# A Mamba time-step projection widened to 128 rows, and eight SiLU gates put into later steps

## The chip, the core and the metric

The kernel runs on one core of one Trainium2 chip. A core has five engines that run side by side and meet through semaphores: TensorE (matmuls; PE in the profile, its weight loads PEld), VectorE (DVE), ScalarE (ACT), GpSimd (POOL) and SyncE (SP), which here only starts DMAs. Each engine works off its own list of instructions in order. Matmul results land in PSUM[...]; all other tiles lie in SBUF, over 128 partitions. The metric is the device time of one execution in microseconds (us).

## What is computed

A layer of three parts on 16 sequences of 128 rows and 512 features, in float32: cross-attention over 2048 context rows per sequence, a Mamba block with an MLP, and an FFN with a gate. The change touches the Mamba block alone. Cut to what matters:

```python
xz = einsum('bld,ed->ble', Z, in_proj_w)
x, z = split(xz, 2)                        # 1024 channels each
x = silu(causal_conv(x, conv_w, conv_b))
dt, Bm, Cm = split(einsum('bld,ed->ble', x, x_proj_w), [32, 48])
dt = softplus(einsum('blr,dr->bld', dt, dt_proj_w) + dt_proj_b)
h = exp(dt * A) * h + dt * Bm * x          # scanned over the 128 rows, 16 states a channel
y = (h . Cm) + x * D
y = y * silu(z)
out = einsum('bld,ed->ble', y, out_proj_w)
```

The time-step projection, `dt_proj_w`, contracts over 32 values only.

## The kernel before

**Steps.** One loop over `u` runs the whole kernel (L1151 to L1221 of the file). A step of the attention phase, `u` from 0 to 255, handles one sequence, one of four context blocks of 512 rows and one of four groups of four heads. There are 256 of them; the tail, `u` from 256 on, does the rest of the Mamba work and the FFN. The order in which a step issues its instructions is written by hand, and each engine keeps it:

1. DMA loads; the first half of the scan decays (`decays(g, r, 0)`, ScalarE).
2. `scores` (TensorE, four matmuls of 32 rows each at four places of the array, into the four banks), then `weighted` of the step before (TensorE), `maxima` (VectorE, L306), `x_products` (TensorE, L236), `exps` (ScalarE, L316).
3. Inputs of the next step's scan (GpSimd, L631) and sums of context blocks (`t1` to `t4`, GpSimd, L228); `silu_third`; first half of the scan (VectorE: L666, L669, and L645 which clears the state's first column); second half of the decays (L652), which waits for that clearing.
4. `turn`: 16 transposes of the exponentials (TensorE, L329) into the four banks, copied out as `pT` by ScalarE (banks 0, 1 and 3, L334) and VectorE (bank 2, L332); second half of the scan.
5. The lists `middle`, `late`, `after` and `inner`: work that is put at a given step. An item of `late` uses TensorE and gets a bank, the first one bank 0, the second bank 1, and so on; it must wait until `pT` has been copied out of that bank, and the next step's scores must wait until its result has been read.
6. `y_products` (TensorE, L236) and their sums; `silu_second` (VectorE).

**Mamba work.** Sequences are taken in pairs, the groups `g` from 0 to 7. Group `g` starts from p = 32 (g + 1). Its input projection for channel block `ec` (eight blocks of 128) stands in `late` at step p + 9 + ec: `x_part` with its convolution and `z_part`. `x_proj` follows at p + 18 and writes `xd`, 64 rows: the 32 time-step rows, then B and C, which go to DRAM by a DMA (L573). From p + 22 (the constant `LAG`) the group's 32 scan steps run, four for each channel block, so from step 54 on every step holds a scan. The time-step projection of block `ec` (`dt_first`, L593) stands in `late` at p + 19 + 4 ec: a matmul with the weight tile `dtw` (32 rows, loaded by `load_dtproj` one step earlier) and the first 32 rows of `xd`. Then ScalarE reads its bank (L602) and VectorE as well (L605). Since groups are 32 steps apart, the same work returns at the same number of the step modulo 32: the projections at 19, 23, 27, 31, 3, 7, 11 and 15.

**SiLU.** It is made of exp and log, in three pieces. `silu_first` (list `after`): Abs, Exp, Ln on ScalarE (L550 to L552). `silu_second` at the same step's end: one VectorE operation (L557). `silu_third` in the next step: an Exp on ScalarE (L561) and a product on GpSimd (L562). Both gates of a block, of x and of z, are put at p + 10 + ec. The x gates must be done before `x_proj`; a z gate is needed only when the scan of its block is over, at the end of step p + 25 + 4 ec (L687).

Of the kernel before, what the change touches and what calls it, by code (L numbers as in the profile page):

```python
# [8 lines left out]
FP = mybir.dt.float32  # L9
# [6 lines left out]
P = 128  # L16
# [4 lines left out]
DI, DS, DTR = 1024, 16, 32  # L21
# [4 lines left out]
GT = GB * NQ  # L26
# [8 lines left out]
def perceiver_layer(ctx: ExitStack, tc: tile.TileContext, a: dict, out: bass.AP):  # L35
    nc = tc.nc
# [21 lines left out]
    bcd = [dram.tile([2 * DS, GT], FP, tag=f"bcd{g}", name=f"bcd{g}") for g in range(B // GB)]  # L58
# [5 lines left out]
    def moments(pool, dst, src):  # L64
        st = pool.tile([P, 6], FP, tag="st", name="st", bufs=4)
        nc.vector.bn_stats(st, src)
        nc.vector.bn_aggr(dst, st)
# [36 lines left out]
    NG = B // GB  # L104
    NU = B * SB * 4
    LAG = 22
    NF = B // MB
    with ExitStack() as es:
        acon = es.enter_context(tc.tile_pool(name="acon", bufs=1))
        keep = es.enter_context(tc.tile_pool(name="keep", bufs=2))  # L110
        ssm = es.enter_context(tc.tile_pool(name="ssm", bufs=2))
# [64 lines left out]
        def reload_x(b):  # L176
            t = keep.tile([P, D], FP, tag="x", name=f"xn{b}", bufs=4)
            nc.sync.dma_start(t, xnd[b])
            xts[b] = t
# [295 lines left out]
        dskip = acon_in("dskip", [P, EC])  # L475
        aneg = acon_in("alog", [P, EC, DS])

        zTs, xas, zss, xds, bcs, dts, wts, ysum, wts_in = ({} for _ in range(9))
        sgs = []

        def bt(t):
# [2 lines left out]
        def load_win(g, i):  # L484

            t = ssm.tile([P, KC, P], FP, tag="ws", name=f"win{g}_{i}", bufs=WS)
            nc.sync.dma_start(t, a["win"][i // 4][:, :, (i % 4) * P : (i % 4 + 1) * P])
            wts_in[g, i] = t
# [29 lines left out]
        def x_part(g, ec, ps):  # L518


            ps = ps[:, 0:GT]
            in_proj(g, ec, ps)
            t = ssm.tile([P, GT], FP, tag="xa", name=f"xa{g}_{ec}", bufs=10)
            nc.scalar.activation(
                t, ps, AF.Identity, bias=convb[:, ec : ec + 1], scale=convw[:, ec, 3:4]
            )
            for k in (2, 1, 0):
                s = 3 - k
                nc.vector.scalar_tensor_tensor(
                    bt(t)[:, :, s:],  # L530
                    bt(ps)[:, :, 0 : NQ - s],
                    convw[:, ec, k : k + 1],
                    bt(t)[:, :, s:],
                    ALU.mult,
                    ALU.add,
                )
            xas[g, ec] = t

        def z_part(g, ec, ps):
            ps = ps[:, 0:GT]  # L540
            in_proj(g, EC + ec, ps)
            t = ssm.tile([P, GT], FP, tag="zs", name=f"zs{g}_{ec}", bufs=16)
            nc.scalar.copy(t, ps)
            zss[g, ec] = t

        def silu_first(g, ec, ts):

            v = ts[g, ec]
            t = ssm.tile([P, GT], FP, tag="sg", name="sg", bufs=4)
            nc.scalar.activation(t, v, AF.Abs)  # L550
            nc.scalar.activation(t, t, AF.Exp, scale=-1.0)
            nc.scalar.activation(t, t, AF.Ln, bias=1.0)  # L552
            sgs.append((v, t))
# [11 lines left out]
        def x_proj(g, ps):  # L565
            ps = ps[0 : DTR + 2 * DS, 0:GT]
            for ec in range(EC):
                nc.tensor.matmul(
                    ps, xproj[:, ec, :], xas[g, ec], start=(ec == 0), stop=(ec == EC - 1)
                )  # L570
            xd = ssm.tile([DTR + 2 * DS, GT], FP, tag="xd", name=f"xd{g}", bufs=1)
            nc.vector.tensor_copy(xd, ps)
            nc.sync.dma_start(bcd[g], xd[DTR:, :])  # L573
            xds[g] = xd

        def load_bc(t, base):

# [7 lines left out]
                )  # L585
                bcs[t, base] = x

        def load_dtproj(g, ec):
            t = ssm.tile([DTR, P], FP, tag="dtw", name=f"dtw{g}_{ec}", bufs=1)
            nc.sync.dma_start(t, a["dtproj"][:, ec * P : (ec + 1) * P])  # L590
            dts[g, ec] = t

        def dt_first(g, ec, ps):  # L593

            ps = ps[:, 0:GT]
            nc.tensor.matmul(
                ps, dts[g, ec], xds[g][0:DTR, :], start=True, stop=True
            )


            e = ssm.tile([P, GT], FP, tag="e", name="e", bufs=1)
            nc.scalar.activation(e, ps, AF.Abs, bias=dtb[:, ec : ec + 1])  # L602
            nc.scalar.activation(e, e, AF.Exp, scale=-1.0)
            dt = ssm.tile([P, GT], FP, tag="dt", name="dt")
            nc.vector.tensor_scalar(dt, ps, dtb[:, ec : ec + 1], 0.0, ALU.add, ALU.max)  # L605
            u = ssm.tile([P, GT], FP, tag="u", name="u", bufs=1)
            nc.gpsimd.tensor_scalar(u, e, 1.0, 1.0, ALU.mult, ALU.add)
            dts[g, ec] = dt, e, u

        def dt_second(g, ec):  # L610
            dt, e, u = dts[g, ec]
            nc.vector.scalar_tensor_tensor(e, u, 1.0, e, ALU.subtract, ALU.subtract)
            l = ssm.tile([P, GT], FP, tag="l", name="l", bufs=1)
            nc.scalar.activation(l, u, AF.Ln)
            dts[g, ec] = dt, e, l
# [23 lines left out]
        def states(g, r, i):  # L639

            return pc if i and 32 * (g + 1) + LAG + r >= NU - 2 else hst

# [47 lines left out]
        def projected(g, i, ps):  # L690
# [14 lines left out]
            moments(keep, mvz[:, b, :], x)  # L705
            if b // MB == NF - 1:
                xrs[b] = x
# [274 lines left out]
        def call(f, *xs):  # L982
            return lambda: f(*xs)
# [10 lines left out]
        def hidden_units(m):  # L994
            for q in range(4):
                unit([call(load_wf, m, 1, q)], [call(hidden, m, q)], [call(gelus, m, q)])
            if m:
                units[-4][2].append(call(mlp_norm, m - 1, both))
                units[-3][2].append(call(last_norm, m - 1, both))
                units[-1][1].insert(0, call(x_turned, m - 1, both))  # L1000
# [7 lines left out]
        def second_units(m):  # L1008
            for q in range(4):
                unit([call(load_wf, m, 2, q)], [call(second, m, q)])  # L1010
            units[-4][3].append(call(load_x1, m))
            units[-2][2].append(call(with_b2, m))
            if m < NF - 1:
                units[-1][2].append(call(mlp_sum, m, both))
# [12 lines left out]

        for m in range(NF - 1):
            hidden_units(m)
            if m:  # L1030
                expert_units(m - 1)
            second_units(m)
            if m < NF - 2:
                units[-4][3].append(call(load_z, m + 1))
# [7 lines left out]
        feeds = len(units) - 1  # L1042
        m = NF - 1
        units[-1][1].append(call(z_norm, m))
# [12 lines left out]
        late, after, inner, middle, loads = ({} for _ in range(5))  # L1057

        def put(where, u, f):
            where.setdefault(u, []).append(f)  # L1060

        for b in range(B):
            s = 16 * b
# [20 lines left out]
        for g in range(NG):  # L1084
            p = 32 * (g + 1)
            for ec in range(EC):
                put(loads, p + 8 + ec, lambda g=g, ec=ec: load_win(g, ec))
                put(loads, p + 8 + ec, lambda g=g, ec=ec: load_win(g, EC + ec))
                put(late, p + 9 + ec, lambda ps, g=g, ec=ec: x_part(g, ec, ps))
                put(late, p + 9 + ec, lambda ps, g=g, ec=ec: z_part(g, ec, ps))  # L1090
                put(after, p + 10 + ec, lambda g=g, ec=ec: silu_first(g, ec, xas))
                put(after, p + 10 + ec, lambda g=g, ec=ec: silu_first(g, ec, zss))
            put(late, p + 18, lambda ps, g=g: x_proj(g, ps))
            s = p + LAG
            for ec in range(EC):
                put(loads, s - 4 + 4 * ec, lambda g=g, ec=ec: load_dtproj(g, ec))
                put(late, s - 3 + 4 * ec, lambda ps, g=g, ec=ec: dt_first(g, ec, ps))
                put(middle, s - 2 + 4 * ec, lambda g=g, ec=ec: dt_second(g, ec))
                put(inner, s - 2 + 4 * ec, lambda g=g, ec=ec: dt_third(g, ec))
            for i in range(GB):  # L1100
                for ec in range(WS):
                    put(loads, s + 32 + 2 * i, lambda g=g, i=i, ec=ec: load_wout(g, i, ec))
                put(loads, s + 31 + 2 * i, lambda b=g * GB + i: reload_x(b))
                put(late, s + 33 + 2 * i, lambda ps, g=g, i=i: projected(g, i, ps))
# [32 lines left out]
        ps = banks[2]  # L1137
# [10 lines left out]

        last = 32 * NG + LAG + 32 + 4
        fed = 0  # L1150
        for u in range(last):  # L1151
            live = u < NU
            g, r = divmod(u - 32 - LAG, 32)
            scans = 0 <= g < NG
# [3 lines left out]
            of, phase = ("k", "v")[phase // 2], phase % 2  # L1158
            load_bc(u + 2 - 32 - LAG, 0)
            if u % 4 == 1 and made + 1 < B * SB:  # L1160
# [7 lines left out]
            if u > NU:  # L1168
                while fed < feeds * (u - NU) // (last - 1 - NU):
                    feed(fed)  # L1170
                    fed += 1
            load_bc(u + 1 - 32 - LAG, DS)
            if u == NU + 1:
# [124 lines left out]
```

## Time and profile before

| | us |
|---|---|
| median of 3 runs | 3945.24 (3941.79 to 3951.43) |
| the profiled execution | 3947.16 |
| its span, first to last instruction | 3945.4 |
| attention phase, first to last step's scores | 55.8 to 3184.0 |
| tail | 3184.0 to 3945.4 |

The mean granted TensorE clock was 0.987 of full speed. Busy time by stretch:

| stretch (us) | TensorE | VectorE | ScalarE | GpSimd |
|---|---|---|---|---|
| 0 to 56 | 38.1 | 18.1 | 7.5 | 18.9 |
| 56 to 700 (no scans at first) | 641.9 | 317.6 | 375.3 | 127.2 |
| 700 to 3184 | 2437.3 | 1934.0 | 1725.5 | 1568.0 |
| 3184 to 3945 | 694.0 | 457.8 | 307.1 | 388.8 |

A step's length, from its first score matmul to the next step's, is nearly the same in every group, to a few hundredths of a microsecond. The steps that the change touches, in the third group's cycle (steps 96 to 127), beside the same place in the first group's (32 to 63), where no scan runs until step 54:

| step modulo 32 | 32 to 63 | 96 to 127 | | step modulo 32 | 32 to 63 | 96 to 127 |
|---|---|---|---|---|---|---|
| 3 | 10.08 | 10.97 | | 16 | 14.39 | 15.38 |
| 7 | 9.21 | 10.28 | | 17 | 9.21 | 9.21 |
| 10 | 14.39 | 14.78 | | 18 | 14.76 | 16.88 |
| 11 | 13.10 | 13.92 | | 20 | 11.81 | 12.57 |
| 12 | 17.96 | 18.95 | | 21 | 9.21 | 9.21 |
| 13 | 12.66 | 13.08 | | 23 | 10.28 | 16.91 |
| 14 | 14.39 | 15.68 | | 24 | 11.47 | 11.47 |
| 15 | 12.66 | 13.48 | | 25 | 9.21 | 16.09 |

How to read the profile's rows: a group has line, engine, operation, output and inputs, shape and count, then busy time and mean ns of one, then the engine's idle time just before these instructions and what ended it. A timeline row has start, length, engine, line, operation, tiles, and how many instructions in a row were merged into it; in brackets stand the idle time before it and its releaser. "Issue" is idle time that no wait in the profile explains. A matmul's row ends when its last result is out, and matmuls overlap, so the rate at which TensorE works is the distance from start to start: 0.109 us for 128 columns and 0.216 us for 256, in every place where nothing is waited for.

### The profile page before, as it was taken

How to read it: one execution, taken by the hardware profiler on the slowest of the kernel's cores; microseconds unless marked ns; L12 is line 12 of the kernel's file. 1: busy time of each engine (PE TensorE's matmuls, PEld its weight loads, DVE VectorE, ACT ScalarE, POOL GpSimd, SP SyncE). 2: the span in 40 equal slices, each digit the busy share in tenths (PEclk: the TensorE clock that was granted, in tenths of full speed). 3: DMA queues.
4: the chain of work that ended last, by engine and by line, in shares of the span. 5: the costliest groups of instructions: out<-in, count | busy, mean ns of one | idle time of the engine just before them, and what ended most of it. 6: DMA issues, size and time to landing. Idle time of an engine off the chain costs nothing.

```text
span 3945.4 us, 70725 instructions
## 1 busy us (share of the span) xinstructions
PE 3811.3 (97%) x26120; PEld 2871.7 (73%) x26120; DVE 2727.5 (69%) x4898; ACT 2415.4 (61%) x5799; POOL 2102.8 (53%) x1968
## 2 busy tenths in 40 slices
PE   7999999999999999999999999999999989989998
PEld 6878787777777777777777777777777756655654
DVE  3444445887778777877787778777877776767732
ACT  3555566767667766776677756775777654534421
POOL 1111213775667565666566657665765575656710
PEclk9999999999999999999999999999999989999999
DMA  2111212444444434443444353535443466567641
GB/s 90 41 39 41 62 54 95 133 150 123 152 150 143 140 130 157 146 140 127 164 136 152 111 172 125 162 113 170 130 156 106 167 232 219 185 236 264 216 169 59
DMA packets 341225, 548.42 MB, mean 139 GB/s; under 512 B 24432, under 2 KB 225408, under 8 KB 340624
## 3 DMA queue, kind: packets, MB, share of 16 engines
q1 hardware_dynamic: 340464, 543.28, 42.2%
q8 instruction: 206, 3.38, 0.4%
q14 instruction: 139, 1.14, 0.1%
q0 software_dynamic: 416, 0.63, 0.1%
HBM read 527.29 MB, written 16.52 MB: 138 GB/s over the span
## 4 chain that ended last, share of the span: by engine, by line
PE 72%; DVE 13%; ACT 10%; issue 2%; DMA 2%; POOL 1%; SPq 0%; DVEq 0%; ACTq 0%; POOLq 0%
PE pa L236 17%; PE pc L236 13%; PE bank L329 8%; PE bank L298 6%; PE bank L514 6%; PE avp L342 5%; PE bank L695 3%; ACT pr L316 3%; DVE hst L666 3%; DVE nm L306 3%; ACT hst L652 2%; DVE w L669 2%; PE bank L394 2%; PE bank L460 2%; PE bank L855 1%
## 5 line engine op out<-in xcount | busy, mean ns | idle before, releaser
L682 POOL TENSOR_TENSOR ysum<-ysum,w 128x512 f32<-128x512 f32 x384 | 500.1, 1302 | 645.6 <-DVE hst L645 309.0
L306 DVE TENSOR_REDUCE nm<-bank 128x1 f32<-128x512 f32 x1024 | 635.3, 682 | 253.5 <-PE bank L298 252.6
L316 ACT ACTIVATE pr<-bank,nm 128x512 f32<-128x512 f32 x1024 | 690.6, 688 | 101.3 <-DVE nm L306 95.4
L631 POOL TENSOR_TENSOR w<-dx,bc 128x512 f32<-128x512 f32 x512 | 651.3, 1293 | 4.1 <-DMA bc<-bcd 0.3
L666 DVE TENSOR_TENSOR_SCAN hst<-hst,w 128x512 f32<-128x512 f32 x456 | 556.8, 1221 | 2.7 <-ACT hst L652 2.7
L652 ACT ACTIVATE hst<-dt,alog 128x254 f32<-128x254 f32 x912 | 437.1, 479 | 174.7 <-DVE hst L645 152.0
L329 PE MATMUL bank<-ident,pr 128*128 128x128 f32 x4096 | 498.8, 275 | 14.0 <-ACT pr L316 14.0
L329 PEld LDWEIGHTS bank<-ident,pr 128*128 128x128 f32 x4096 | 467.5, 142 | 45.9 <-ACT pr L316 19.7
L334 ACT COPY pT<-bank 128x512 f32<-128x512 f32 x768 | 402.4, 586 | 60.8 <-PE bank L329 60.6
L342 PEld LDWEIGHTS avp<-pT,v 128*32 128x32 f32 x8192 | 208.2, 110 | 200.7 <-issue 193.7
L669 DVE TENSOR_TENSOR w<-hst,bc 128x512 f32<-128x512 f32 x456 | 315.3, 692 | 48.0 <-DMA bc<-bcd 32.8
L298 PE MATMUL bank<-kt,qT 32*128 32x512 f32 x2048 | 304.0, 640 | 3.2 <-DVE dt L605 2.6
L228 POOL TENSOR_TENSOR t<-c,c 128x512 f32<-128x512 f32 x128 | 164.5, 1286 | 251.0 <-PE pc L236 242.9
L342 PE MATMUL avp<-pT,v 128*32 128x128 f32 x8192 | 278.8, 276 | 5.3 <-DVE v L266 5.3
L514 PE MATMUL bank<-zT,win 128*128 128x256 f32 x1024 | 237.5, 385 | 16.5 <-ACT pT L334 11.4
L236 PE MATMUL pa<-t,ks 128*128 128x256 f32 x1024 | 248.4, 385 | 1.4 <-ACT u2ku L276 1.4
L236 PE MATMUL pa<-vs,t 128*128 128x256 f32 x1008 | 248.8, 390 | 0.0
L332 DVE COPY pT<-bank 128x512 f32<-128x512 f32 x256 | 176.7, 690 | 99.1 <-PE bank L329 97.3
L514 PEld LDWEIGHTS bank<-zT,win 128*128 128x128 f32 x1024 | 190.8, 191 | 53.2 <-ACT pT L334 19.9
L236 PEld LDWEIGHTS pa<-vs,t 128*128 128x128 f32 x1008 | 182.3, 190 | 45.7 <-issue 23.1
L236 PEld LDWEIGHTS pa<-t,ks 128*128 128x128 f32 x1024 | 186.0, 190 | 37.7 <-issue 9.2
L316 ACT ACTIVATION_READ_ACCUMULATOR pr<-bank,nm 128x1 f32 x1024 | 210.1, 205 | 0.0
(268 smaller groups left out, 6831.8 us busy)
## 6 DMA issues: line engine op xcount, KB each, us to landing
bc<-bcd SPq DMA_DIRECT2D x512, 512.0 KB, 4.4
c<-in_ctxT_dram SPq DMA_DIRECT2D x256, 256.0 KB, 4.4
wf<-in_w_dram SPq DMA_DIRECT2D x128, 512.0 KB, 7.3
wqo<-in_wqkvo_dram SPq DMA_DIRECT2D x128, 256.0 KB, 4.9
win<-in_win_dram SPq DMA_DIRECT2D x128, 256.0 KB, 4.7
wout<-in_wout_dram SPq DMA_DIRECT2D x128, 256.0 KB, 4.0
x<-in_x_dram SPq DMA_DIRECT2D x16, 256.0 KB, 3.7
x1d<-x SPq DMA_DIRECT2D x16, 256.0 KB, 2.2
```

The lines of the kernel that those rows point to most:

```text
L236: nc.tensor.matmul(ps[:, r, :], l[:, kc, r * P : (r + 1) * P], m[:, kc, :], start=(i in (1, 2, 5) and r == 0 and kc == 0), stop=(r == 1 an ...
L298: nc.tensor.matmul(banks[j], qts[b][rows, hg, :], kts[u // 4, hg][rows, :], start=True, stop=True)
L306: nc.vector.tensor_reduce(stats[b][0][j][:, sb, hg : hg + 1], banks[j], AX.X, ALU.max, negate=True)
L316: nc.scalar.activation(pr[:, j, :], banks[j], AF.Exp, bias=nm[j][:, sb, hg : hg + 1], accum_out=sm[:, sb, h : h + 1],)
L329: nc.tensor.transpose(ps[:, j, :], prs[u][:, j, i * P : (i + 1) * P], ident)
L334: nc.scalar.copy(pT, ps)
L342: nc.tensor.matmul(avp[j * HD : (j + 1) * HD, hg, :], vts[u // 4, hg // 2, i // 2][:, i % 2, hg % 2 * P + j * HD : hg % 2 * P + (j + 1) * HD],
L514: nc.tensor.matmul(ps, w[:, kc, :], zTs[g][:, kc, :], start=(kc == 0), stop=(kc == KC - 1))
L631: nc.gpsimd.tensor_tensor(w, dx.unsqueeze(1).to_broadcast([P, NH // 2, GT]), bcs[g * 32 + r, 0][:, i * NH // 2 : (i + 1) * NH // 2, :], AL ...
L652: nc.scalar.activation(bt(h[:, k, :])[:, :, 1:], bt(dt)[:, :, 1:], AF.Exp, scale=aneg[:, ec, n : n + 1],)
L666: nc.vector.tensor_tensor_scan(flat, flat, w.rearrange("p n t -> p (n t)"), 0.0, ALU.mult, ALU.add)
L682: nc.gpsimd.tensor_tensor(s, s, w, ALU.add)
```

## The change

Two edits. The first makes `xd` and `dtw` tiles of 128 rows that are made once, before the loops, and cleared once (two VectorE memsets). `x_proj` copies into the first 64 rows of `xd`, and the weight load fills the first 32 rows of `dtw`; the projection's matmul takes all 128 rows of both. Rows 32 to 127 of `dtw` stay zero, so rows 32 to 63 of `xd`, which hold B and C, add nothing. The second edit puts the z gates, which stood at p + 10 to p + 17, at p + 20, 22, 23, 24, 25, 36, 38 and 40 for the blocks 0 to 7; the last three fall on the steps 4, 6 and 8 of the next cycle of 32. The x gates stay.

```diff
+    Z_GATES = (20, 22, 23, 24, 25, 36, 38, 40)
...
-            xd = ssm.tile([DTR + 2 * DS, GT], FP, tag="xd", name=f"xd{g}", bufs=1)
-            nc.vector.tensor_copy(xd, ps)
-            nc.sync.dma_start(bcd[g], xd[DTR:, :])
-            xds[g] = xd
+            nc.vector.tensor_copy(xd[0 : DTR + 2 * DS, :], ps)
+            nc.sync.dma_start(bcd[g], xd[DTR : DTR + 2 * DS, :])
...
-        def load_dtproj(g, ec):
-            t = ssm.tile([DTR, P], FP, tag="dtw", name=f"dtw{g}_{ec}", bufs=1)
-            nc.sync.dma_start(t, a["dtproj"][:, ec * P : (ec + 1) * P])
-            dts[g, ec] = t
+
+        xd = ssm.tile([P, GT], FP, tag="xd", name="xd", bufs=1)
+        dtw = ssm.tile([P, P], FP, tag="dtw", name="dtw", bufs=1)
+        nc.vector.memset(xd, 0.0)
+        nc.vector.memset(dtw, 0.0)
+
+        def load_dtproj(ec):
+            nc.sync.dma_start(dtw[0:DTR, :], a["dtproj"][:, ec * P : (ec + 1) * P])
...
-            nc.tensor.matmul(
-                ps, dts[g, ec], xds[g][0:DTR, :], start=True, stop=True
-            )
+            nc.tensor.matmul(ps, dtw, xd, start=True, stop=True)
...
-                put(after, p + 10 + ec, lambda g=g, ec=ec: silu_first(g, ec, zss))
+                put(after, p + Z_GATES[ec], lambda g=g, ec=ec: silu_first(g, ec, zss))
...
-                put(loads, s - 4 + 4 * ec, lambda g=g, ec=ec: load_dtproj(g, ec))
+                put(loads, s - 4 + 4 * ec, lambda ec=ec: load_dtproj(ec))
```

The line numbers in the prediction are those of the kernel before.

More of the change, by code (lines that the diff above doesn't have):

```diff
@@ L476, in perceiver_layer @@
         aneg = acon_in("alog", [P, EC, DS])
-        zTs, xas, zss, xds, bcs, dts, wts, ysum, wts_in = ({} for _ in range(9))
+        zTs, xas, zss, bcs, dts, wts, ysum, wts_in = ({} for _ in range(8))
         sgs = []
```

## The prediction

> **What bounds the kernel now.** I read the page's busy shares first, then the groups by shape, then the timeline of single steps; a step's place is its number modulo 32.
>
> ```profile
> PE 3811.3 (97%) x26120; PEld 2871.7 (73%) x26120; DVE 2727.5 (69%) x4898; ACT 2415.4 (61%) x5799; POOL 2102.8 (53%) x1968
> ```
>
> TensorE bounds the span, but inside single steps another engine can end last, so a TensorE saving counts only where TensorE arrives last. The 64 time-step projections are 128 matmuls (fp32 runs each in two passes):
>
> ```profile
> L596 PE MATMUL bank<-xd,dtw 32*128 32x256 f32 x128 | 44.9, 430 | 1.1 <-DVE aT L452 1.1
> L596 PEld LDWEIGHTS bank<-xd,dtw 32*128 32x128 f32 x128 | 18.9, 184 | 19.3 <-issue 12.3 <-ACT pT L334 4.2 <-DVE aT L452 1.3
> L514 PE MATMUL bank<-zT,win 128*128 128x256 f32 x1024 | 237.5, 385 | 16.5 <-ACT pT L334 11.4 <-ACT hs L839 3.0 <-DVE dt L605 1.3
> L514 PEld LDWEIGHTS bank<-zT,win 128*128 128x128 f32 x1024 | 190.8, 191 | 53.2 <-ACT pT L334 19.9 <-issue 4.3 <-ACT hs L839 3.4
> ```
>
> The 19.3 us of idle before the L596 weight loads is large for 128 loads. The timeline of step 51 shows it (start, length, engine, line, count):
>
> ```profile
> 627.66 0.59 PE L236 MATMUL pc<-va,c 128*128 128x256 f32 x2
> ...
> 629.84 1.04 PE L447 MATMUL bank<-ident,fx 128*128 128x128 f32 x8
> ...
> 630.80 0.29 PEld L596 LDWEIGHTS bank<-xd,dtw 32*128 32x128 f32 x2 [0.17 <-issue]
> 630.80 0.69 PE L596 MATMUL bank<-xd,dtw 32*128 32x256 f32 x2
> ...
> 631.42 1.59 PEld L236 LDWEIGHTS pa<-vs,t 128*128 128x128 f32 x8 [0.33 <-issue]
> 631.43 1.99 PE L236 MATMUL pa<-vs,t 128*128 128x256 f32 x8
> ```
>
> Two full-height matmuls in a row take 0.59 us, that is one start-to-start of 0.216 plus the last one's 0.379; the 32-row pair takes 0.69 (0.320 + 0.374). Eight full-height ones take 1.89 elsewhere, but 1.99 here, right after the 32-row pair.
>
> **Part 1, the padding, on TensorE.** Four pieces per projection: entry, 630.80 less the last L447 start (629.84 + 7 x 0.109 = 630.60) is 0.20 against 0.109: 0.094 with all digits. Between the pair: 0.320 - 0.216 = 0.104. Exit, 630.80 + 0.32 to 631.43 is 0.304 against 0.216: 0.088. First L236 start-to-start afterwards: 1.99 - 1.89 = 0.104. Sum **0.39 us**, x 64 = 25 us. The matmuls before and after all 64 are full-height (128 rows, 128 columns), so after the change no switch is left at either side.
>
> Here a rule speaks against the change. The Trainium skill, TensorE: Matmul & The Clock Gate, section "Why this matters for your kernels", says that one K=32 matmul takes as long as a K=128 one, the gain of small K being concurrent tiles; that makes padding worth 0. The durations agree (374 against 379, loads 184 against 190 ns), the start-to-start distances don't (0.320 against 0.216). I take the row, 25 us on TensorE, and keep 0 as the other end. The switch itself fits TensorEngine Tiling (Array Packing), "Key Properties": changing the mode drains the array.
>
> How much passes on? Step 103 (place 7):
>
> ```profile
> 1260.01 1.22 DVE L666 TENSOR_TENSOR_SCAN hst<-hst,w 128x512 f32<-128x512 f32 x1
> ...
> 1261.27 0.69 DVE L669 TENSOR_TENSOR w<-hst,bc 128x512 f32<-128x512 f32 x1
> ...
> 1262.00 0.48 DVE L605 TENSOR_SCALAR dt<-bank,dtb 128x256 f32<-128x256 f32 x1
> ...
> 1262.53 0.31 PEld L298 LDWEIGHTS bank<-kt,qT 32*128 32x128 f32 x8 [0.59 <-DVE dt L605]
> ```
>
> The next scores need the bank that L605 reads, and L605 stands behind pT, scan and product on VectorE, which hang on the step's transposes, not on the projection. So here TensorE waits already, and 0.39 less work is 0.39 more wait: gain 0. I looked at all 51 projections of steps 51 to 251 in this way. Places 7 and 31 wait 0.25 us now; at places 3, 19 and 27 one of the four scores waits 0.3 to 0.6: gain 0. Places 11 and 15 have 3 us to spare: 0.39 each, 6 groups x 2 = 4.7. Place 23 has 0.33 to spare: 6 x 0.33 = 2.0. Step 51, before the scans, 0.4. Attention phase: **7.1 us**. The 13 projections from step 255 on run between full-height FFN matmuls: up to 5.1; several stretches there end on a GELU or a norm, so I take **3**.
>
> The two memsets stand in the first 56 us, where VectorE is busy 18.1: 0 (a 128x512 copy of 0.69 each if that cover failed). DMAs, their order on SP, and every wait of the projection are unchanged; the wider copies carry no more columns.
>
> **Part 2, SiLU of z.** Each z gate is three ScalarE operations (0.40 + 0.42 + 0.42), one VectorE (L557, 0.43 alone, 0.86 mean), a fourth ScalarE one (0.42; 0.30 more in a row) and one GpSimd (0.73) in the next step. Nothing vanishes; it leaves places 10 to 18. Step 110 (place 14) shows the price there:
>
> ```profile
> 1347.40 1.14 PE L298 MATMUL bank<-kt,qT 32*128 32x512 f32 x8
> ...
> 1348.68 0.88 DVE L557 SCALAR_TENSOR_TENSOR sg<-zs,sg 128x256 f32<-128x256 f32 x1 [0.55 <-ACT sg L552]
> ...
> 1349.48 2.47 DVE L306 TENSOR_REDUCE nm<-bank 128x1 f32<-128x512 f32 x4
> ...
> 1353.04 1.91 PE L329 MATMUL bank<-ident,pr 128*128 128x128 f32 x16
> ...
> 1355.98 0.48 PE L514 MATMUL bank<-zT,win 128*128 128x256 f32 x1 [1.03 <-ACT pT L334]
> ```
>
> The scores end at 1348.54, but the maxima start at 1349.48, behind z's L557; maxima, exps, second scan decays and pT copies are one chain, and L514 waits for the first copy. It could start at 1353.04 + 16 x 0.109 = 1354.79: stall 1.19. Stalls behind the transposes, now and after (us):
>
> - Place 12: 0.88 to 0.34. Places 8 and 24 have the same rows without SiLU and their first copy ends 0.01 before the transposes; x's fourth operation adds 0.30.
> - 13: 0.32 to 0 (15 carries two fourth operations without loss once the maxima are on time).
> - 14: 1.19 to 0.29, what places 6, 10 and 22 show without SiLU.
> - 16: 0.89 to 0.34, as 12.
> - 18: 0.43 + 1.47 (wait for the bank of x_proj) to 1.03: the maxima come 0.87 earlier and no more, since the softmax join of place 17 is still ahead.
> - 24, new: 0 to 0.31, the z fourth operation ahead of the copy that z_turned waits for.
>
> Gain 0.54 + 0.32 + 0.90 + 0.55 + 0.87 - 0.31 = 2.87 per group. The first group has no such stall (no scans yet), the last lies in the tail; 6 x 2.87 = **17.2 us**.
>
> At the other receiving places the cover is this: in 5, 7, 9, 21, 23 and 25 VectorE ends its earlier work about 1.2 us or more before the scores are done, more than z's L557; the fourth operation lies in ScalarE's wait for the scan state; place 26 has 0.1 to spare on VectorE but no late work behind a bank. GpSimd's product queues behind the sums t1 to t4, so the t2 that TensorE needs is on time except for 0.73 later at 25, where 2 us are to spare. Bounds: 0 each, or 0.3 at 7, 9, 23 and 25, which is 4 x 0.3 x 7 = 8 us lost. I take 0. In the tail, the z gate at 3303 stands before the GELU that a 5.2 us stall at 3307 waits for: gain at most 1.25, I take **1**; x_proj's 4.1 us stall at 3415 waits behind a GELU and two w products on GpSimd, which stay.
>
> **Sum.** 7.1 + 3 + 17.2 + 1 = 28 us. The profiled execution took 3947.16 (span 3945.4), the median is 3945.24; from the median **3917 us**.
>
> **Rivals.** (A) The forecast, 3917, own range 3905 to 3930: 0.66. (B) Everything passes on, because VectorE's chain moves up too: 25 + 6 x 5.5 (all excess of places 10 to 18) = 58, 3887. For it: TensorE at 97%; against it: L605 above. 0.08. (C) The chain keeps its time through other rows: VectorE's scan memset, not z, sets the copies, so only 14 and 18 gain about 1 us together, and the padding 4 us: 10 us, 3935. For it: x keeps its L557 in each of these steps. 0.14. (D) Slower: z's L557 at its new places again lies between scores and maxima, as in step 110, at 1.19 in eight places of seven groups: 67 lost less 28 gained, about 3984. It decides once L557 ends over about 1 us behind the scores where late work waits for a bank; only 24 (0.04 us to spare on VectorE) comes near, and there ScalarE starts its exps late anyway. 0.05. (E) Padding does nothing, as the rule says: 18 us left, 3927. 0.07.
>
> Range **3900 to 3937**: A and E inside, most of C. About 12 us (0.3%) is what a measurement of this kernel tells from no change. Faster: A, B, E and a third of C, 0.85; same: the rest of C and a little of D, 0.11; slower 0.04.
>
> **What would show it.** The projection's pair at 0.59 us with no switch idle before it and eight L236 at 1.89 after it; at places 7 and 31 the wait for L605 grown to about 0.6 with the step's length unchanged; places 11 and 15 shorter by 0.39; place 14 with its stall at 0.3, place 18 at 1.0, place 24 longer by 0.3. Wrong would be: a pair still 0.69, places 12 to 18 unchanged, or stalls at 23, 25, 7 or 9.

## The result and the profile after

The changed kernel takes 3929.44 us, median of 5 runs (3925.23 to 3931.51); the kernel before took 3946.66 in 5 runs beside them. The ratio is 0.9953, with a 95% interval of 0.9939 to 0.9968: faster by 17 us, where 28 were forecast. The time lies inside the predicted range. From here on lines of the new kernel are named. They are one higher than before (the scores, L298, are now L299), except the time-step projection, L596, which is now L599. A step's place is its number modulo 32.

The busy shares of the page, after:

```profile
PE 3791.6 (97%) x26120; PEld 2877.2 (73%) x26120; DVE 2736.4 (70%) x4900; ACT 2416.6 (62%) x5799; POOL 2102.8 (54%) x1968
```

Shares of busy time hardly differ from before, so the answer must be in single steps. The groups by shape show the padded projection:

```profile
L599 PE MATMUL bank<-xd,dtw 128*128 128x256 f32 x128 | 39.2, 388 | 0.3 <-DVE aT L453 0.3
...
L599 PEld LDWEIGHTS bank<-xd,dtw 128*128 128x128 f32 x128 | 20.4, 189 | 6.4 <-issue 5.0 <-DVE aT L453 0.6 <-DVE pc L667 0.2
```

A load takes 189 ns as it did with 32 rows (184), but the idle time ahead of these loads is 6.4 us in all instead of 19.3. The timeline of step 51 after, to be read against the same step in the prediction (start, length, engine, line, count):

```profile
632.80 1.04 PE L448 MATMUL bank<-ident,fx 128*128 128x128 f32 x8
...
633.67 0.60 PE L599 MATMUL bank<-xd,dtw 128*128 128x256 f32 x2
...
634.11 1.89 PE L237 MATMUL pa<-vs,t 128*128 128x256 f32 x8
```

The last L448 starts at 632.80 + 7 x 0.109 = 633.56, the first L599 0.11 later, the first L237 0.44 = 2 x 0.22 after that, and the eight L237 take 1.89 instead of 1.99. The four start-to-starts of the forecast were 0.203, 0.320, 0.304 and 0.320; they are now 0.109, 0.226, 0.216 and 0.216: 0.38 saved, 0.39 forecast.

Whether a step gets it is seen at step 103 (place 7), after:

```profile
1260.43 1.22 DVE L667 TENSOR_TENSOR_SCAN hst<-hst,w 128x512 f32<-128x512 f32 x1
...
1261.69 0.69 DVE L670 TENSOR_TENSOR w<-hst,bc 128x512 f32<-128x512 f32 x1
...
1262.42 0.48 DVE L606 TENSOR_SCALAR dt<-bank,dtb 128x256 f32<-128x256 f32 x1
...
1262.96 0.31 PEld L299 LDWEIGHTS bank<-kt,qT 32*128 32x128 f32 x8 [0.96 <-DVE dt L606]
```

The step's length is unchanged (10.28 us). The score weights' wait for L606 grew from 0.59 to 0.96: TensorE came 0.38 earlier and waited that much longer, because scan and product still stand ahead of L606. (Of both waits 0.33 is the "issue" idle that these loads have where no engine is waited for, as in the timeline of both below; so the wait proper grew from 0.26 to 0.63, and about 0.6 was forecast.)

Place 14 (step 110), where z's L557 stood between scores and maxima:

```profile
1346.54 1.14 PE L299 MATMUL bank<-kt,qT 32*128 32x512 f32 x8
1347.70 2.48 DVE L307 TENSOR_REDUCE nm<-bank 128x1 f32<-128x512 f32 x4 [0.73 <-PE bank L299]
...
1352.18 1.91 PE L330 MATMUL bank<-ident,pr 128*128 128x128 f32 x16
...
1354.22 1.99 PE L515 MATMUL bank<-zT,win 128*128 128x256 f32 x8
```

The maxima now wait for the scores alone, and L515 starts 0.30 us after it could (1352.18 + 16 x 0.109 = 1353.92), where it was 1.19.

The place that took back part of what others gave is the start of place 24 (step 120). Before:

```profile
1482.46 1.14 PE L298 MATMUL bank<-kt,qT 32*128 32x512 f32 x8
...
1483.62 2.48 DVE L306 TENSOR_REDUCE nm<-bank 128x1 f32<-128x512 f32 x4
...
1488.04 0.06 DVE L645 MEMSET hst<- 128x4 f32 x1
...
1488.29 1.03 ACT L652 ACTIVATE hst<-dt,alog 128x254 f32<-128x254 f32 x2
...
1489.25 1.55 ACT L334 COPY pT<-bank 128x512 f32<-128x512 f32 x3
```

After:

```profile
1478.56 1.20 PE L299 MATMUL bank<-kt,qT 32*128 32x512 f32 x8
...
1479.22 0.66 DVE L499 TENSOR_SCALAR x<-x,mv,rstd 128x512 f32<-128x512 f32 x1
...
1479.80 1.49 DVE L558 SCALAR_TENSOR_TENSOR sg<-zs,sg 128x256 f32<-128x256 f32 x1
...
1481.22 2.47 DVE L307 TENSOR_REDUCE nm<-bank 128x1 f32<-128x512 f32 x4
1481.93 0.69 ACT L317 ACTIVATE pr<-bank,nm 128x512 f32<-128x512 f32 x1 [0.51 <-DVE nm L307]
...
1483.61 1.21 DVE L667 TENSOR_TENSOR_SCAN hst<-hst,w 128x512 f32<-128x512 f32 x1
...
1485.63 0.06 DVE L646 MEMSET hst<- 128x4 f32 x1
...
1485.78 0.99 ACT L653 ACTIVATE hst<-dt,alog 128x254 f32<-128x254 f32 x2 [0.28 <-DVE hst L646]
...
1486.71 1.54 ACT L335 COPY pT<-bank 128x512 f32<-128x512 f32 x3
```

The scores are done at 1479.76, but z's L558 sits ahead of the maxima and takes 1.49 us, so the maxima start 2.66 us into the step (before: 1.16). VectorE takes maxima, first scan half, product and the clearing of the state (L646) one after the other; the second decays (L653) now wait for that clearing, and the pT copies follow on ScalarE. They start 8.15 us into the step instead of 6.79, and the step is 1.35 us longer (1.21 in one of the six groups).

Summed over the attention phase (first scores to the last step's scores), read from step lengths against before:

| places | us each | sum |
|---|---|---|
| 11, 15 | -0.33 | -4.0 |
| 23 | -0.39 | -2.3 |
| 19 and 3 | -0.39, and +0.39 in the step that follows | 0 |
| step 51 | -0.39 | -0.4 |
| 7, 27, 31 | 0.00 | 0 |
| 12, 13, 14, 16, 18 | -0.54, -0.41, -0.90, -0.54, -0.87 | -19.6 |
| 24 | +1.35 (one group +1.21, the first +0.30) | +8.2 |
| 26 of the first group, 29 and 30 of the last | +0.54; -0.39, -0.21 | -0.1 |

Together -18.3, which is what the phase lost (3128.24 to 3109.91). The -0.39 at 29 of the last group is chance: before_again has it too. The first scores came 3.1 us later and the tail took 1.2 less, so the span fell by 16.5.

### The profile page after: what moved, and what is told of

The parts are those of the page before. It is cut to its first block, busy times and chain, and to the rows that moved or that the text cites. A ratio compares the mean times of both kernels' runs of the same rounds, so it can differ in the third digit from the quotient of the medians.

```text
span 3928.9 us, 70620 instructions
## 1 busy us (share of the span) xinstructions
PE 3791.6 (97%) x26120; PEld 2877.2 (73%) x26120; DVE 2736.4 (70%) x4900; ACT 2416.6 (62%) x5799; POOL 2102.8 (54%) x1968
## 4 chain that ended last, share of the span: by engine, by line
PE 72%; DVE 16%; ACT 6%; issue 3%; DMA 2%; POOL 1%; SPq 0%; DVEq 0%; ACTq 0%; POOLq 0%
PE pa L237 18%; PE pc L237 13%; PE bank L330 8%; PE bank L299 7%; PE bank L515 6%; PE avp L343 5%; DVE hst L667 4%; DVE nm L307 4%; DVE w L670 2%; ACT hst L653 2%; PE bank L696 2%; PE bank L395 2%; PE bank L461 2%; PE bank L856 2%; PE bank L826 1%
## 5 line engine op out<-in xcount | busy, mean ns | idle before, releaser
L632 POOL TENSOR_TENSOR w<-dx,bc 128x512 f32<-128x512 f32 x512 | 646.5, 1284 | 3.8
L653 ACT ACTIVATE hst<-dt,alog 128x254 f32<-128x254 f32 x912 | 437.1, 479 | 163.7 <-DVE hst L646 143.0
L330 PEld LDWEIGHTS bank<-ident,pr 128*128 128x128 f32 x4096 | 464.9, 142 | 42.6 <-ACT pr L317 16.4
L299 PE MATMUL bank<-kt,qT 32*128 32x512 f32 x2048 | 310.6, 643 | 11.4 <-DVE dt L606 7.9
L237 PE MATMUL pa<-t,ks 128*128 128x256 f32 x1024 | 249.8, 387 | 0.0
L237 PE MATMUL pa<-vs,t 128*128 128x256 f32 x1008 | 244.7, 386 | 0.0
L515 PE MATMUL bank<-zT,win 128*128 128x256 f32 x1024 | 235.6, 383 | 7.6 <-ACT hs L840 4.6
L515 PEld LDWEIGHTS bank<-zT,win 128*128 128x128 f32 x1024 | 191.4, 191 | 39.6 <-ACT pT L335 8.0
L237 PEld LDWEIGHTS pa<-t,ks 128*128 128x128 f32 x1024 | 187.0, 191 | 36.5 <-issue 11.8
L237 PEld LDWEIGHTS pa<-vs,t 128*128 128x128 f32 x1008 | 185.5, 190 | 34.8 <-issue 12.3
```

The costliest lines, as they stand in the source:

```text
L237: nc.tensor.matmul(ps[:, r, :], l[:, kc, r * P : (r + 1) * P], m[:, kc, :], start=(i in (1, 2, 5) and r == 0 and kc == 0), stop=(r == 1 an ...
L299: nc.tensor.matmul(banks[j], qts[b][rows, hg, :], kts[u // 4, hg][rows, :], start=True, stop=True)
L330: nc.tensor.transpose(ps[:, j, :], prs[u][:, j, i * P : (i + 1) * P], ident)
L515: nc.tensor.matmul(ps, w[:, kc, :], zTs[g][:, kc, :], start=(kc == 0), stop=(kc == KC - 1))
L632: nc.gpsimd.tensor_tensor(w, dx.unsqueeze(1).to_broadcast([P, NH // 2, GT]), bcs[g * 32 + r, 0][:, i * NH // 2 : (i + 1) * NH // 2, :], AL ...
L653: nc.scalar.activation(bt(h[:, k, :])[:, :, 1:], bt(dt)[:, :, 1:], AF.Exp, scale=aneg[:, ec, n : n + 1],)
```

## The experiments

Each profile gives three parts: the start (up to the first scores), the attention phase, the tail. The phase repeats to within a microsecond (before_again), the other two do not, so mechanisms are judged on the phase.

| run | us | ratio to before, 95% | start | attention, against before | tail |
|---|---|---|---|---|---|
| before | 3946.66 | | 55.8 | 3128.24 | 761.4 |
| after | 3929.44 | 0.9953 (0.9939 to 0.9968) | 58.9 | -18.33 | 760.1 |
| pad_only | 3941.82 | 0.9986 (0.9977 to 0.9995) | 59.5 | -5.66 | 757.9 |
| z_only | 3935.72 | 0.9967 (0.9956 to 0.9978) | 57.7 | -12.65 | 760.7 |
| second_later | 3926.99, one run | | 58.8 | -23.72 | 761.9 |
| gate_moved | 3921.84 | 0.9933 (0.992 to 0.9947) | 57.1 | -24.91 | 759.2 |
| tail_old | 3924.34 | 0.9944 (0.9931 to 0.9958) | 58.0 | -25.63 | 760.3 |
| pad64 | 3925.46, one run | | 58.1 | -19.05 | 756.4 |
| scan_later | 3923.6 | 0.9938 (0.9926 to 0.9951) | 58.0 | -23.72 | 761.8 |
| before_again | 3949.62, one run | | 57.7 | -0.77 | 762.7 |
| both | 3905.84 | 0.988 (0.9864 to 0.9897) | 59.8 | -43.93 | 762.1 |
| both32 | 3921.49 | 0.9927 (0.9913 to 0.9941) | 57.5 | -30.64 | 765.0 |

**The two parts apart.** The padding alone (pad_only):

```diff
-            t = ssm.tile([DTR, P], FP, tag="dtw", name=f"dtw{g}_{ec}", bufs=1)
...
+        xd = ssm.tile([P, GT], FP, tag="xd", name="xd", bufs=1)
+        dtw = ssm.tile([P, P], FP, tag="dtw", name="dtw", bufs=1)
...
+            nc.tensor.matmul(ps, dtw, xd, start=True, stop=True)
```

> The padding alone; both SiLU gates stay at p + 10 + ec. My theory (TensorE gains 0.39 us per projection, and it passes on only where VectorE's L605 is not last): the attention phase is 6.7 us shorter than before (0.33 to 0.39 at places 11, 15 and 23 in six groups each, nothing net at 3, 7, 19, 27, 31), the tail 0 to 5, so 0.997 to 0.9985 of the time before. Rival (all of TensorE's saving passes on): 25 us, 0.9937. Rival (the page's rule, padding is worth nothing): 1.000.

And the later z gates alone, with the projection over 32 rows (z_only):

```diff
+    Z_GATES = (20, 22, 23, 24, 25, 36, 38, 40)
...
-                put(after, p + 10 + ec, lambda g=g, ec=ec: silu_first(g, ec, zss))
+                put(after, p + Z_GATES[ec], lambda g=g, ec=ec: silu_first(g, ec, zss))
```

> The later z gates alone; the projection stays at 32 rows. My theory: places 12 to 18 gain 3.27 us per group (19.6 in six groups), place 24 loses 1.35 in six groups and 0.3 in one, and 0.5 at one place 26: the attention phase is 10 us shorter, with the tail 0.997 to 0.998 of before. Rival (the two parts help each other): less than 6 us in the attention phase. The first scores start at 55.8 us as before if the two memsets are what made them start at 58.9; if they start anywhere between 55 and 59 the start is chance.

The phase lost 5.66 with the padding (11 -0.30, 15 -0.33, 23 -0.39 a group, one lone +1.16 at one place 24) and 12.65 with the gates (the five places as after, 24 +1.16, one 26 +0.53). 5.66 + 12.65 = 18.31 against 18.33 together, but that the sum comes out so well is luck. At place 24 the padding alone costs 0.06, the gates alone 1.16, and both together 1.35: the padding starts that step 0.39 earlier, while VectorE's work ahead of z's operation does not come earlier by as much (the operation starts 1.24 into the step, 1.04 in z_only). The lone +1.16 in pad_only hides this in the sum. There no gate is in the way; the norm L499 is late and takes 1.53 us, and the maxima start 2.46 into the step all the same (step 184):

```profile
2291.72 1.55 PE L299 MATMUL bank<-kt,qT 32*128 32x512 f32 x8
...
2292.74 1.53 DVE L499 TENSOR_SCALAR x<-x,mv,rstd 128x512 f32<-128x512 f32 x1
...
2294.18 2.47 DVE L307 TENSOR_REDUCE nm<-bank 128x1 f32<-128x512 f32 x4
```

So late VectorE work ahead of the maxima makes this step over a microsecond longer even without a gate. The padding's gain is small, but its interval excludes none.

**What makes place 24 longer.** Two things were new there: z's VectorE operation ahead of the maxima, and z's fourth ScalarE operation ahead of the decays and copies, the only one that the forecast had priced (0.31). The next kernel issues that one VectorE operation after the maxima and leaves everything else (second_later):

```diff
+            if u % 32 == 24 and live:
+                silu_second()
...
-            silu_second()
+            if u % 32 != 23 or not live:
+                silu_second()
```

> The changed kernel, but the VectorE piece of the gate that stands at place 23 (L557) is issued one step later, behind the maxima of place 24. Theory 1 (place 24 loses because that piece waits behind the norm of place 23 and holds up the maxima): the maxima of place 24 start 1.2 us after the step's start again, the step takes 11.8 us instead of 12.82, the attention phase is 6 us shorter than in the changed kernel. Theory 2 (the gate's three ScalarE operations at the end of place 23 delay the copies of place 24): still 12.6 or more.

The timeline of the same steps in second_later:

```profile
1477.47 1.20 PE L299 MATMUL bank<-kt,qT 32*128 32x512 f32 x8
...
1478.70 2.47 DVE L307 TENSOR_REDUCE nm<-bank 128x1 f32<-128x512 f32 x4
1480.23 0.69 ACT L317 ACTIVATE pr<-bank,nm 128x512 f32<-128x512 f32 x1
...
1481.10 0.41 DVE L558 SCALAR_TENSOR_TENSOR sg<-zs,sg 128x256 f32<-128x256 f32 x1
1481.43 1.22 DVE L667 TENSOR_TENSOR_SCAN hst<-hst,w 128x512 f32<-128x512 f32 x1
...
1483.45 0.06 DVE L646 MEMSET hst<- 128x4 f32 x1
1483.66 1.03 ACT L653 ACTIVATE hst<-dt,alog 128x254 f32<-128x254 f32 x2
...
1484.62 1.55 ACT L335 COPY pT<-bank 128x512 f32<-128x512 f32 x3
```

The maxima start 1.23 into the step, L558 takes 0.41 instead of 1.49, the decays do not wait for L646, and the copies start at 7.15. Place 24 is 0.36 longer than before instead of 1.35. So 0.99 of it is the VectorE operation standing ahead of the maxima. The other 0.36 is what is left with the fourth ScalarE operation in place (and L558 between maxima and scan); the padding alone has 0.06 of it, which leaves 0.30, near the 0.31 forecast.

**Another place for that gate.** If place 23 alone is bad, no gate should stand there (gate_moved):

```diff
-    Z_GATES = (20, 22, 23, 24, 25, 36, 38, 40)
+    Z_GATES = (20, 22, 24, 25, 28, 36, 38, 40)
```

> The changed kernel with the z gates at p + 20, 22, 24, 25, 28, 36, 38, 40: none at place 23. Theory 1: place 24 is back at 11.47 us, place 29 stays at 9.21 (VectorE is done 0.9 us before its start there), so the attention phase is 9 us shorter than in the changed kernel and the whole about 0.993 of before. Theory 2 (the work comes back wherever it is put): place 29 or 25 loses about what 24 gains, 0.995.

Place 24 is +0.05 against before, 26 +0.14 (and +0.83 in the first group), 29 0.00; the phase is 6.6 us shorter than after, where 9 were expected. The loss belonged to the place, not to the later gates.

**The tail.** The last group's z gates put back to p + 10 + ec, on top of gate_moved (tail_old):

```diff
-                put(after, p + Z_GATES[ec], lambda g=g, ec=ec: silu_first(g, ec, zss))
+                put(after, p + (Z_GATES[ec] if g < NG - 1 else 10 + ec), lambda g=g, ec=ec: silu_first(g, ec, zss))
```

> gate_moved, but the last group's z gates, which run in the tail, stand at p + 10 + ec as before. Theory (the later gates cost the tail what the padding gives it): the tail takes 758 us as with the padding alone, 1 to 2 us less than gate_moved's 759.2. Rival (the tail's differences are chance): within 1 us of 759.2 either way. My forecast's step (moving them gains 1 us there): 760 or more.

The tail took 760.3 against 759.2, and the intervals of the ratios overlap: not resolved. Over all profiles the tail lies between 756.4 and 765.0 in no order of the edits; the mean is 762.4 over four with a 32-row projection and 760.5 over seven with 128 rows, which leans the forecast's way (3 us) but is no more than the spread.

**Half the rows.** gate_moved with the projection over 64 rows (pad64):

```diff
-            nc.tensor.matmul(ps, dtw, xd, start=True, stop=True)
+            nc.tensor.matmul(ps, dtw[0:64, :], xd[0:64, :], start=True, stop=True)
```

> gate_moved with the projection over 64 rows instead of 128 (the weight's rows 32 to 63 are zero). Theory 1 (any height below 128 is another mode of the array): the pair of matmuls takes 0.69 us again, with 0.17 and 0.33 us of switch idle around it, and places 11, 15 and 23 are 0.33 to 0.39 longer than in gate_moved. Theory 2 (only the 32-row mode pays): the pair at 0.59 us and no switch.

Groups by shape, pad64:

```profile
L599 PE MATMUL bank<-xd,dtw 64*128 64x256 f32 x128 | 44.5, 428 | 1.7 <-DVE aT L453 1.7
...
L599 PEld LDWEIGHTS bank<-xd,dtw 64*128 64x128 f32 x128 | 18.8, 184 | 19.9 <-issue 12.7 <-ACT pT L335 3.7 <-DVE aT L453 2.0
```

19.9 us of idle ahead of the loads and start-to-starts of 0.203, 0.320, 0.306 and 0.320: 64 rows pay what 32 did, and the phase is 5.85 us longer than with 128. What costs is the change of height, and it costs as much at 64 rows as at 32.

**Where the rest of the padding's gain stays.** On TensorE it is 0.38 at each of 51 projections in the phase, 19.4 us, of which 6.7 came through. L606, which the next scores wait for, stands behind the second scan half on VectorE. In scan_later that half is issued behind the late work in every fourth step, on top of gate_moved:

```diff
-            if scans:
+            early = not live or u % 4 != 3
+            if scans and early:
                 scan(g, r, 1)
...
+            if scans and not early:
+                scan(g, r, 1)
```

> gate_moved, and in every fourth step of the attention phase (places 3, 7, ..., 31) the second scan half is issued behind the late work, so that VectorE reads the projection's bank (L605) before the scan and not after it. Theory (L605's place in VectorE's list is what swallows the padding's gain): places 7 and 31 fall from 10.28 to about 9.64 us, the scores behind places 3, 19 and 27 stop waiting; up to 25 us less in the attention phase than gate_moved, less what the later scan costs the next step. Rival (the scan state is on the chain as well, its decays stand ahead of the exps): the next steps, places 0, 4, 8, ..., lose as much as these gain, 0 us or a loss.

Against gate_moved: 4 and 20 -0.86 each, 7 and 31 -0.63, 27 -0.43, 28 -0.29, 26 -0.14; but 8 +1.96 and 24 +2.14, so that the phase is 1.2 us longer. Theory and rival were both partly right: the scan does hold these steps up, and it doesn't vanish by being moved. Timeline of scan_later at the start of place 8 (step 104):

```profile
1258.57 1.22 DVE L667 TENSOR_TENSOR_SCAN hst<-hst,w 128x512 f32<-128x512 f32 x1
1258.88 1.14 PE L299 MATMUL bank<-kt,qT 32*128 32x512 f32 x8
1259.83 0.69 DVE L670 TENSOR_TENSOR w<-hst,bc 128x512 f32<-128x512 f32 x1
...
1261.30 0.91 DVE L499 TENSOR_SCALAR x<-x,mv,rstd 128x512 f32<-128x512 f32 x1
1262.14 2.47 DVE L307 TENSOR_REDUCE nm<-bank 128x1 f32<-128x512 f32 x4
```

Here scan, product and the norm that belongs to this place stand ahead of the maxima, which start 3.26 us into the step (gate_moved: 1.16). At places 0, 4, 20 and 28 no norm stands there. That suggests to move the scan at 3, 19, 27 and 31 only (both):

```diff
-            early = not live or u % 4 != 3
+            early = not live or u % 32 not in (3, 19, 27, 31)
```

> Gates at (20, 22, 24, 25, 28, 36, 38, 40) and, in steps 3, 19, 27 and 31 of every 32 in the attention phase alone, the second half of the scan issued after the late work instead of before the middle. Theory 1 (at these four steps the dt add waits only because the scan stands ahead of it on VectorE, so that moving the scan lets the padding's gain through, and the loss of the run before, +1.96 and +2.14 us at 8 and 24, belongs to the scans moved in steps 7 and 23): against gate_moved 0.86 less at 4, 0.86 at 20, 0.7 at 27 and 28 together, 0.6 at 31, some 3 us a group or 17 to 19 us in six, the attention phase some 43 us shorter than before, ratio about 0.989. Theory 2 (a moved scan delays the copies or maxima of the step that follows wherever it is moved, so that what 4, 20, 28 gain is lost one or two steps later): under 5 us less than gate_moved, ratio 0.992 to 0.994.

The phase is 19.0 us shorter than gate_moved and 43.9 shorter than before, with 0.00 at 8 and 24: the first theory's size, place by place (4 and 20 -0.86, 27 and 28 -0.72 together, 31 -0.63). Timeline of both, end of place 3 (step 99):

```profile
1208.83 0.60 PE L599 MATMUL bank<-xd,dtw 128*128 128x256 f32 x2
...
1209.98 0.48 DVE L606 TENSOR_SCALAR dt<-bank,dtb 128x256 f32<-128x256 f32 x1
...
1210.38 1.22 DVE L667 TENSOR_TENSOR_SCAN hst<-hst,w 128x512 f32<-128x512 f32 x1
1211.09 0.31 PEld L299 LDWEIGHTS bank<-kt,qT 32*128 32x128 f32 x8 [0.33 <-issue]
1211.09 1.14 PE L299 MATMUL bank<-kt,qT 32*128 32x512 f32 x8
```

L606 comes before the scan, and the next scores no longer wait for VectorE ("issue" stands where step 103 above has L606). At 3905.84 us, this version is the fastest of the study.

**Was it the padding that came through?** The same kernel with the 32-row projection (both32):

```diff
-            nc.tensor.matmul(ps, dtw, xd, start=True, stop=True)
+            nc.tensor.matmul(ps, dtw[0:DTR, :], xd[0:DTR, :], start=True, stop=True)
```

> The run before (gates moved, scans of steps 3, 19, 27 and 31 behind the late work) with the projection over 32 rows again, so that it differs from it in the padding alone. Theory 1 (the padding's 0.39 us was lost at 3, 19, 27 and 31 only because the scan stood ahead of the dt add): 0.3 to 0.39 us longer at each of 3 or 4, 11, 15, 19 or 20, 23, 27 or 28 and 31, nothing at 7, where the scan is not moved: 6 x 7 x 0.36 = 15 us more in the attention phase than with the padding, against 5.66 for the padding alone in the kernel before. Theory 2 (the scan's move made these steps shorter by itself, and what the padding saves there is still waited for): the same 6 us as before, from 11, 15 and 23.

It takes 13.3 us more in the phase: 0.39 at 3, 19 and 23, 0.33 at 11, 15 and 27, 0.38 at 31, 0.00 at 7, and 0.05 to 0.10 given back at 4, 20, 24 and 28. So the same padding is worth 5.7 us in the kernel before and 13.3 us here: the TensorE time was always saved, and the scan's place decided whether a step got it. Most of what both gained over gate_moved is the moved scans' own: both32 is 11.6 us shorter in the phase than pad64, which has the same gates and pays the same switches; the padding adds the other 7.4.

**Chance.** The kernel before, unchanged, profiled a second time (before_again):

> The kernel before, unchanged, for a second profile of it. If the start of the first scores is chance, it lies somewhere in 55 to 59.5 us; if the two memsets make it late, it is at 55.8 again. Every step of the attention phase should repeat to some hundredths of a microsecond, the tail within 1 to 2 us of 761.4.

The phase differs by 0.77, the start by 1.9 and the tail by 1.3. Starts lie between 55.8 and 59.8 over all profiles, and z_only (57.7) has no memsets. The 3.1 us later start of after is not theirs; VectorE in after:

```profile
5.55 0.27 DVE L590 MEMSET xd<- 128x256 f32 x1
5.80 0.17 DVE L591 MEMSET dtw<- 128x128 f32 x1
13.07 0.23 DVE L1122 TENSOR_SCALAR alog<-alog 128x128 f32<-128x128 f32 x1 [7.11 <-ACT alog L1121]
```

Behind them it idles 7.11 us. What the starts do go with is the granted clock, shown in the last section.

## Why the prediction was right, and what it mis-sized

**Sign and mechanism.** Faster, inside the range, and the likeliest case was the right one. The time alone would not say so: 3929 is nearer to rival E (3927) than to the forecast (3917), and 3.1 us of the profiled run come from the start, which varies. The single places decide. The padding was right on TensorE (0.38 against 0.39) and in what passes on: 11, 15, 23 and step 51 gave 6.7 us against 7.1 in the phase, and 3, 7, 19, 27 and 31 gave nothing. 11 and 15 gave 0.33, not 0.39; why was not traced. At 19 and 3 the step itself did get shorter and the next one longer by the same; only the sum was as forecast.

The rule weighed there, of the Trainium skill, "TensorE: Matmul & The Clock Gate", section "Why this matters for your kernels" (one K=32 matmul takes as long as one with K=128), holds for the durations here (184 against 189 ns a load) and not for their distance from full-height neighbours. It would have made the padding worth 0. pad_only, 5.66, and both against both32, 13.29, decide for the row. The Trainium skill's "TensorEngine Tiling (Array Packing)", section "Key Properties", has the mechanism without a size (a change of tiling mode drains the array); pad64 agrees with it, as 64 rows pay what 32 do, but no run looks into the array.

**The gates.** The relief at 12, 13, 14, 16 and 18 was 0.54, 0.41, 0.90, 0.54 and 0.87, 19.6 us in six groups against 19.1 forecast (0.54, 0.32, 0.90, 0.55, 0.87). Places 5, 7, 9, 21, 25 and, but for one group, 26 cost nothing, as said.

**The term that failed** is place 24, set at +0.31 and measured at +1.35. Over the phase it lost 8.2 us where 6 x 0.31 = 1.9 were forecast: 6.4 of the 28 us. The prediction had the right suspect in its rival on the slow side (z's L557 between scores and maxima again; "only 24 (0.04 us to spare on VectorE) comes near") and let it go with "there ScalarE starts its exps late anyway". Two things were wrong in that clause. It looked at one consumer of the maxima, the exps; but the first scan half, its product and the clearing L646 stand behind the maxima on the same engine, and L646 releases the second decays ahead of the pT copies. Before, the clearing was done 0.19 ahead of the decays' start; that was all the slack there was. And it took L557 for 0.43 to 0.86, while at that place it takes 1.49, beside a GpSimd product (L632 in the new kernel). second_later shows the 0.99, gate_moved that the rest of the edit does not need it.

**The tail**, forecast at 4 us, measured 1.2, is open: runs of the same kernel differ by as much. **The start** came 3.1 us late, but not through the memsets, which were rightly put at nothing. From 28.3 (the forecast before rounding): less 6.4 at place 24, less 2.8 for the tail, less 3.1 at the start, and +0.4 of small terms gives 16.4; the profiled spans differ by 16.5.

Of the rivals, B (all passes on) falls by step 103; C (other rows keep the chain) by places 12 to 18; E (padding worth nothing) by pad_only; D was right about its mechanism at one place of eight, where it cost 0.99 rather than 1.19.

## What to carry to other kernels

A matmul pair of another height between full-height ones costs 0.38 us here that stands in no row's duration, only in start-to-start distances; zero rows remove it. Whether the time moves depends on what the step's last wait is, so look for the work that is queued ahead of that wait and move it in the same change (5.7 us became 13.3). When work is put into a step that "has room", follow every consumer queued behind it on its engine and not the nearest one alone, and price it with the longest duration that the trace shows for it, not the mean. Judge a change of a few microseconds on the part of the trace that repeats.

## What the hardware showed beside this

**VectorE beside GpSimd.** L558 reads two tiles from SBUF. In the trace of after, the 22 of its 128 instances that lie for less than half of their time beside a GpSimd operation took 0.41 to 0.45 us; the other 106 took 0.41 to 1.53, 0.91 in the mean. The Trainium skill, "SBUF — State Buffer", section "SBUF: two separate sides", says that GpSimd and a VectorE operation with two SBUF inputs take one port pair from each other, whole instructions at a time. The two lengths at place 24 fit it (1.49 while L632 runs up to 1481.01; 0.41 in second_later, when GpSimd is idle), but the port itself was not tested. L499, which reads one such tile, varies too: beside L632 it took 0.66 us in step 120 of after and 1.53 in step 184 of pad_only.

**The clock near the start.** Stretch of 24.4 to 31.0 us; the columns are the stretch, its length, busy time and instructions of TensorE, its loads, VectorE, ScalarE and GpSimd, granted clock, DMA share, GB/s. After:

```profile
24.40:31.00 6.60, 6.60 (x17) 5.31 (x18) 0.67 (x1) 1.02 (x2) 0.00 (x0) 0.54 0.00 0
```

And before:

```profile
24.40:31.00 6.60, 6.30 (x29) 5.58 (x30) 1.43 (x3) 1.92 (x4) 0.00 (x0) 1.00 0.00 0
```

TensorE had been idle for 3.72 us up to 24.40 in after, and for 2.49 up to 24.70 in before. At a granted clock of 0.54 it gets 17 matmuls done instead of 29 at 1.00. The starts of the twelve profiles go by the clock of this stretch: 1.00 in before (first scores at 55.8 us); 0.74 to 0.76 in seven (57.1 to 58.1, before_again and z_only, which have no memsets, among them); 0.50 to 0.56 in the other four (58.8 to 59.8). That idle goes along only roughly: 2.49 us in the first, 3.03 to 4.24 in the seven, 3.72 to 4.41 in the four. What makes the clock fall was not tested.
